# The first context's loads, the last groups' additions and the norm rows of a two-layer cross-attention kernel

## The chip, the core and the metric

The kernel runs on one NeuronCore of a Trainium2 chip, in a single launch. The metric is the device time of one execution in microseconds (us). The profile is one execution taken by the hardware profiler; its span runs from the first to the last instruction.

The engines are named as the profile names them: PE is TensorE (PEld its weight loads), DVE is VectorE, ACT is ScalarE, POOL is GpSimd, SP is the engine whose queue issues every DMA here.

## The reference

There are eight sequences of 512 tokens with 512 features (x), and for each a context of 512 rows with 384 features. Four steps are added to x one after the other, each on a layer-normalised x:

```python
# 1  cosine of projected tokens and projected context rows (H = 256); 512x512 per sequence
v = ln(x) @ Wv.T + bv;  t = ctx @ Wt.T + bt
x = x + (v @ t.T) / max(|v| * |t|, 1e-8)
# 2  ternary feed-forward: quantised activations, ternary weights, 512 -> 2048 -> 512
x = x + bit_linear(silu(depthwise_conv3(bit_linear(ln(x), w1))), w2)
# 3  cross-attention with 16 heads of 32
q = ln(x) @ w_q + b_q;  k = ctx @ w_k + b_k;  u = ctx @ w_v + b_v
x = x + softmax(q @ k.T / sqrt(32)) @ u @ w_o + b_o
# 4  gated channel mixing of each token with the one before it
y = ln(x); xr = mix(y, shifted y, mu_r); xk = mix(y, shifted y, mu_k)
x = x + sigmoid(xr @ W_r) * (relu(xk @ W_k) ** 2 @ W_v)
```

All arrays are float32.

## The kernel before

**Who sets the order.** The kernel is written as small generator tasks (`load`, `split_sb`, `evacuate`, `summed` and so on). While the program is built, an `Agenda` plays them against a plan of the machine: a task yields an engine and a cost ("P" TensorE, "V" VectorE, "A" ScalarE, "G" GpSimd, "S" SP's queue), a kind of buffer, or an event, and the planner takes the waiting task with the lowest rank. The order in which the planner starts the work is the order in which each engine's instructions stand in the program; on the chip each engine runs its list in that order and waits on semaphores. So every number of the plan, such as the delay between an engine's end and the next task (`HOP`), can move many instructions. "W" is VectorE work that shares a memory port with GpSimd in the plan: the two take turns there. Where a task offers a list of ways, as `tensor` does for additions (VectorE or GpSimd), the planner picks the one that is least burdened. Almost every VectorE and GpSimd instruction is issued through one wrapper, so the profile puts them all on line 363; the tiles tell them apart. All ordinary loads and stores go through `load` (line 510).

**Buffers.** SBUF is cut into pages ("main", "small"), PSUM into eight banks ("bank"). A kind of buffer has a limit of how many may be held: `b_mm`, the banks of the projections and cosines of step 1, has five.

**Step 1.** For each sequence `b`, `contexts` loads the context (three chunks of 128 features by 512 rows) and splits each chunk into a rounded high part and a low part (`split_sb`: a cast and a subtraction). For the first sequence the three chunks are loaded one by one, each split before the next is asked for. `fronts` loads x, normalises it and transposes it (line 549). `projections` makes the context side with three products for each pair of parts (lines 456 to 458) and then the x side in float32 (line 448). `evacuate` writes the squares and the values, `norms` sums the squares down the features on TensorE (line 877), and `inverse` raises the sums to the power -1/2 on GpSimd. The norms of the context rows stand down the partitions, one column for each 128 rows; `spread` turns them into a row that stands in all partitions, by four transposes of broadcast columns on TensorE (line 605) and a copy on ScalarE (line 608). `cosines` makes the 512x512 products in four banks (line 448); `finish` on VectorE needs that row, scales each bank, adds x and stores the result as x1. Until `finish` has read it, a bank stays held.

`spread` is also called for the scales of step 2, there without the argument that this change sets, and has a second form, chosen with `through`: store the columns to a DRAM tensor `rd`, then load it as one row broadcast to all partitions.

**Step 3.** Attention runs over 32 groups `n` (eight sequences by four groups of four heads). For each, scores are made with the keys on the partitions (line 1480), exponentials taken on ScalarE (line 1488), and `summed` adds up the exponentials of the four key blocks, in two halves of 128x1024, three additions each. `weigh` multiplies by the values (line 1522). The column sums of the added exponentials (line 1540) of group n - 1 stand ahead of the products of group n; those of the last group stand behind them. `finish3` divides and splits, and the output projection follows.

**Step 4** begins under the end of step 3: `mixed` makes the token mixes (a scaling, a scaled addition on VectorE, a cast, a subtraction), `keys4` multiplies them by W_k (lines 456 to 458 again).

The lines of `contexts` and of `summed` that the change touches, and the callers, are these:

Of the kernel before, what the change touches and what calls it, by code (L numbers as in the profile page):

```python
# [12 lines left out]
ALU = mybir.AluOpType  # L13
# [3 lines left out]
P = 128  # L17
B, S, D = 8, 512, 512
# [3 lines left out]
NCX = DCTX // P  # L22
# [7 lines left out]
NS = B * NG  # L30
# [145 lines left out]
class Agenda:  # L176
# [5 lines left out]

    HOP = {"P": 0.2438, "V": 0.12, "A": 0.17, "G": 0.08, "S": 0.1}

    def __init__(self):
        self.now = self.end = self.lane = self.port = 0.0
# [109 lines left out]
    def dispatch(self, engine):  # L298
        if self.wanted[engine] and self.free[engine] <= self.now:
# [9 lines left out]
            self.busy[engine] += cost  # L309
            self.hop = self.HOP[engine]  # L310
            self.me = task
# [63 lines left out]
def f32(ap):  # L375

    return ap.bitcast(F32)


def tile_kernel(tc, x, ctxT, vecs, bo, wvT, wtT, w1T, w2T, wqkvo, wrT, wkT, wv2T, out):  # L380
    nc = tc.nc
    A, T = nc.scalar, nc.tensor
# [39 lines left out]
    ag = Agenda()  # L422
    V, G = Ported(tc, ag, nc.vector), Ported(tc, ag, nc.gpsimd)
# [49 lines left out]
    def tensor(out, a, b, op):  # L473

        n = a.free_size() / 512
        way = yield [("W", 0.07 + 0.53 * n), ("G", 0.16 + 1.07 * n)]
        (V, G)[way].tensor_tensor(out, a, b, op)

    def copy(out, src):

        n = src.free_size() / 512
        way = yield [("W", 0.07 + 0.27 * n), ("A", 0.10 + 0.42 * n)]
        V.tensor_copy(out, src) if way == 0 else A.copy(out, src)  # L483
# [20 lines left out]
    def split_sb(hi, lo, src):  # L504
        yield from copy(hi, src)
        yield from tensor(lo, src, f32(hi), ALU.subtract)

    def load(dst, src):
        yield "S", 0.5
        nc.sync.dma_start(dst, src)  # L510
        yield ag.transfer(src)
# [78 lines left out]
        for t in range(NT):  # L590
            ag.spawn(part(t), ag.me.rank)

    SPR = 0

    def spread(krow, bank, vals, through=None):

        if through is not None:
            yield from store(rd[through].rearrange("(t p) -> p t", p=P), vals)
            row = yield krow
            yield from load(row, rd[through].unsqueeze(0).to_broadcast([P, S]))  # L600
            return row
        ps = yield bank
        yield "P", 0.44
        for t in range(NT):
            T.transpose(ps[:, t, :], vals[:, t : t + 1].to_broadcast([P, P]), ident)
        row = yield krow
        yield "A", 0.48
        A.copy(row, ps.rearrange("p t q -> p (t q)"))  # L608
        ag.give(ps)
        return row  # L610
# [153 lines left out]
    lns, css, vts = {}, {}, {}  # L764
    ln_done = [Event(NT) for _ in range(B)]
    cd_done = [Event() for _ in range(B)]
    cs_done = [Event() for _ in range(B)]
    vt_done = [Event(2 * NHX) for _ in range(B)]
    ns_done = [Event() for _ in range(B)]
    kv_done = [Event(NG + NT) for _ in range(B)]  # L770
# [24 lines left out]
    def contexts():  # L795
        for b in range(B):
            ag.me.rank = (b - LEAD) * T1
            craw = yield k_ctx
            cs = yield k_cs
            css[b] = cs  # L800
            if b > 0:
                yield from load(craw, ctxT[b])
            for c in range(NCX):
                if b == 0:

                    yield from load(craw[:, c, :], ctxT[b, :, c])
                yield from split_sb(cs[c], cs[NCX + c], craw[:, c, :])
            ag.give(craw)
            ag.set(cs_done[b])
            ag.spawn(parked(b, cs), ag.me.rank)  # L810

    def projections():
        yield w_done["t"]
        for b in range(B):
            ag.me.rank = b * T1
            vv = yield k_vv
            vts[b] = vv
            ns, ns_got, sq_done = [], Event(), Event(2)
            for s in (1, 0):
                if s == 1:  # L820
                    yield cs_done[b]
                    (w,), nk, bias, src = wt, NCX, "bt", css[b]
                else:
                    yield w_done["v"]
                    yield ln_done[b]
                    (w,), nk, bias, src = wv, NC, "bv", lns[b][0]
                sqs, both = [], Event(NHX)
                for m in range(NHX):
                    ps = yield b_mm
                    if s == 1:  # L830
                        yield from mac3(ps, lambda c: parts(w, c, tok(m)), lambda c: part2(src, c, ALL), nk)
                    else:
                        yield from mac4(ps, lambda c: w[:, c, tok(m)], lambda c: src[:, c, :], nk)
                    ag.spawn(evacuate(b, s, m, ps, bias, sqs, both), ag.me.rank)
                ag.spawn(norms(s, sqs, both, ns, ns_got, sq_done), ag.me.rank)
                if s == 0:
                    ag.give(src)
                else:
                    ag.spawn(released_when(cd_done[b], src), ag.me.rank)
            ag.spawn(inverse(b, ns, sq_done), ag.me.rank)  # L840

    def parked(b, cs):

        for i in range(2 * NCX):
            yield from store(cd[b, i // NCX, :, i % NCX], f32(cs[i]))
        ag.set(cd_done[b])
# [34 lines left out]
    def inverse(b, ns, sq_done):  # L881
# [14 lines left out]
        V.tensor_scalar(lim, lim, 1e8, None, ALU.mult)  # L896
        rt = yield from spread(k_row, b_pt, rn[:, NT : 2 * NT], (b, 0) if SPR & 1 else None)
        rns[b] = rn, rt, lim
# [365 lines left out]
    R3 = 620.0  # L1264
    T3 = 19.0
    NSTK = 4
    AVK = 2
    MX = 1.6
    GQ = 5
# [14 lines left out]
    k3_xo = main.kind(2, D)  # L1284
    k3_stk = main.kind(2 * NSTK, HG, S, dtype=F32R)
    k3_nmT = small.kind(2, 2, P, dtype=F32R, rows=HG * NT)
# [7 lines left out]
    b3_av = psum.kind(2, S)  # L1294
    free3 = small.kind(NSTK, 1)
    qk_scale = 1.0 / float(HD) ** 0.5
# [15 lines left out]
    def stacks_made():  # L1312


        for i in range(NSTK):
            qs = yield k3_stk
# [63 lines left out]
    def stacks():  # L1380
        yield stks_done
        for n in range(NS):
# [4 lines left out]
            token = yield free3  # L1387
            qs, ks = stks[n % NSTK]
            tokens[n] = token
# [13 lines left out]
    def maxima():  # L1403

        for n in range(NS):
            ag.me.rank = R3 + (n - MX) * T3
            yield loaded[n]
            qs, ks = stks[n % NSTK]
            nmc = yield s3_nmc
# [16 lines left out]
    def lower_rows(n, nmc, done):  # L1426
        qs, ks = stks[n % NSTK]
        yield done
        pt = yield b3_n
        yield "P", 0.15  # L1430
        T.transpose(pt, nmc.rearrange("p j t -> p (j t)"), ident)
        ag.give(nmc)
        nmT = yield k3_nmT
        yield "A", 0.16
        A.copy(nmT[:, 0, :], pt)
        yield "V", 0.16
        V.tensor_tensor(nmT[:, 1, :], pt, f32(nmT[:, 0, :]), ALU.subtract)
        ag.give(pt)
        for a in range(2):
            yield "S", 0.5  # L1440
            nc.sync.dma_start(f32(qs[96 + a : 97 + a]), f32(nmT[:, a, :]))
            wait = ag.transfer(nmT[:, a, :])
        yield wait
        ag.give(nmT)
        ag.set(max_done[n])
# [46 lines left out]
    def summed(n, h, ps, accs):  # L1492

        for k in range(NT):
            ag.me.rank = R3 + (n + (2 * k + h + 1) / 8) * T3
            yield ps[k, h][1]
            if k == 0:
                acc = yield k3_acc
                accs[h] = acc
            else:  # L1500
                yield from tensor(acc, ps[0, h][0] if k == 1 else acc, ps[k, h][0], ALU.add)
                if k == 1:
                    ag.set(ps[0, h][2])
                ag.set(ps[k, h][2])
        ag.set(accs_done[n])

    def weigh(n, av, ps, av_done):
        for first in range(0, NT, AVK):
            both = [(k, h) for k in range(first, first + AVK) for h in range(2)]
            for k, h in both:  # L1510
                yield ps[k, h][1]
            ag.me.rank = R3 + (n + (2 * (first + AVK) - 1) / 8) * T3
            before = n > 0 and first == 0
            if before:
                yield accs_done[n - 1]
                sm = yield b3_w
            yield "P", 0.31 + 0.863 * (AVK + before)
            if before:
                sums(n - 1, sm)
            for k in range(first, first + AVK):  # L1520
                for j in range(HG):
                    T.matmul(  # L1522
                        av[j * HD : (j + 1) * HD, :], vs[n][:, k, j * HD : (j + 1) * HD],
                        ps[k, j // 2][0][:, j % 2, :], start=(k == 0), stop=(k == NT - 1),
                    )
            for k, h in both:
                ag.set(ps[k, h][2])
                ag.spawn(released(*ps[k, h]), ag.me.rank)
        ag.set(av_done)
        ag.give(vs.pop(n))  # L1530
        if n == NS - 1:
            yield accs_done[n]
            sm = yield b3_w
            yield "P", 1.17
            sums(n, sm)
# [307 lines left out]
```

## Time and profile before

| | us |
|---|---|
| three runs | 1606.19, 1607.86, 1610.59 |
| their median | 1607.86 |
| the profiled execution, its time | 1610.36 |
| its span, first to last instruction | 1608.4 |
| PE busy | 1542.0 (96% of the span) |
| DVE busy | 1241.1 (77%) |
| ACT busy | 1090.9 (68%) |
| POOL busy | 671.8 (42%) |
| mean granted TensorE clock | 0.988 |

Busy time is the time in which the engine had an instruction running; register and DMA-issuing instructions do not count. An engine's idle time is put down to what released the instruction after it. The steps overlap: step 1 fills about 0 to 225 us (beside the keys and values of step 3 and the start of step 2), step 2 runs to about 710, attention from about 720 to 1300, step 4 from there to the end.

### The profile page before, as it was taken

How to read it: one execution, taken by the hardware profiler on the slowest of the kernel's cores; microseconds unless marked ns; L12 is line 12 of the kernel's file. 1: busy time of each engine (PE TensorE's matmuls, PEld its weight loads, DVE VectorE, ACT ScalarE, POOL GpSimd, SP SyncE). 2: the span in 40 equal slices, each digit the busy share in tenths (PEclk: the TensorE clock that was granted, in tenths of full speed). 3: DMA queues.
4: the chain of work that ended last, by engine and by line, in shares of the span. 5: the costliest groups of instructions: out<-in, count | busy, mean ns of one | idle time of the engine just before them, and what ended most of it. 6: DMA issues, size and time to landing. Idle time of an engine off the chain costs nothing.

```text
span 1608.4 us, 22301 instructions
## 1 busy us (share of the span) xinstructions
PE 1542.0 (96%) x7552; PEld 987.3 (61%) x7552; DVE 1241.1 (77%) x2044; ACT 1090.9 (68%) x1794; POOL 671.8 (42%) x385
## 2 busy tenths in 40 slices
PE   6999999998999998989999999999999979999998
PEld 4555566655566665656666556555555547878886
DVE  5678899999789989869885887788987555655642
ACT  6686889868778887645766666666676665656551
POOL 1111000000000000133867889988878994544540
PEclk9999999999999999999999999999999989999999
DMA  8898524443444444577666666565765232112101
GB/s 301 309 360 279 180 86 130 151 145 123 159 132 144 148 136 149 191 258 219 183 181 191 177 151 179 144 180 157 197 170 147 74 90 101 52 60 69 69 27 53
DMA packets 133395, 251.48 MB, mean 156 GB/s; under 512 B 22689, under 2 KB 40481, under 8 KB 127138
## 3 DMA queue, kind: packets, MB, share of 16 engines
q1 hardware_dynamic: 133282, 250.06, 49.6%
q8 instruction: 60, 0.98, 0.3%
q14 instruction: 53, 0.43, 0.1%
HBM read 160.88 MB, written 88.34 MB: 155 GB/s over the span
## 4 chain that ended last, share of the span: by engine, by line
PE 68%; DVE 19%; DMA 4%; ACT 4%; issue 3%; POOL 1%; SPq 0%; POOLq 0%; ACTq 0%; DVEq 0%
DVE main L363 15%; PE bank L456 10%; PE bank L457 9%; PE bank L458 9%; PE bank L1480 7%; PE bank L1416 7%; PE bank L1522 6%; PE bank L1218 5%; PE bank L448 4%; DVE small L363 4%; PE bank L442 3%; PE bank L549 2%; PE bank L1540 2%; PE bank L1142 2%; ACT main L1488 1%
## 5 line engine op out<-in xcount | busy, mean ns | idle before, releaser
L363 POOL TENSOR_TENSOR main<-main,main 128x1024 f32<-128x1024 f32 (+3 forms) x316 | 588.5, 1886 | 255.5 <-DVE main L363 96.9
L456 PE MATMUL bank<-main,main 128*128 128x512 f32 x874 | 390.7, 447 | 13.5 <-ACT main L608 3.6
L363 DVE TENSOR_REDUCE small<-bank 128x1 f32<-128x512 f32 (+2 forms) x522 | 330.3, 675 | 89.1 <-PE bank L1416 86.1
L1488 ACT ACTIVATE main<-bank 128x512 f32<-128x512 f32 x512 | 279.4, 604 | 103.2 <-PE bank L1480 99.1
L458 PE MATMUL bank<-main,main 128*128 128x512 f32 x874 | 345.6, 395 | 0.0
L457 PE MATMUL bank<-main,main 128*128 128x512 f32 x824 | 326.3, 396 | 3.5 <-POOL main L363 2.9
L363 POOL TENSOR_TENSOR small<-small,mhalf 128x4 f32<-128x4 f32 (+2 forms) x43 | 51.2, 1191 | 644.8 <-DVE small L363 627.8
L363 DVE TENSOR_TENSOR main<-main,main 128x1024 f32<-128x1024 f32 (+3 forms) x205 | 245.8, 1209 | 16.5 <-ACT main L483 8.0
L456 PEld LDWEIGHTS bank<-main,main 128*128 128x128 f32 x874 | 166.8, 191 | 87.5 <-issue 22.3
L1480 PE MATMUL bank<-main,main 98*128 98x512 f32 x512 | 212.8, 418 | 2.8 <-ACT main L1488 1.2
L1416 PE MATMUL bank<-main,main 96*128 96x512 f32 x512 | 211.2, 414 | 1.5 <-DVE small L363 0.4
L458 PEld LDWEIGHTS bank<-main,main 128*128 128x128 f32 x874 | 165.9, 190 | 37.2
L363 DVE SCALAR_TENSOR_TENSOR main<-bank,vec,main 128x511 f32<-128x511 f32 x254 | 181.5, 740 | 7.8 <-ACT main L1148 7.4
L457 PEld LDWEIGHTS bank<-main,main 128*128 128x128 f32 x824 | 157.7, 191 | 34.1 <-issue 3.9
L442 PE MATMUL bank<-main,main 128*128 128x512 fp8e4 x512 | 134.2, 388 | 3.4 <-ACT main L1124 3.4
L483 ACT CAST main<-main 128x512 fp32r<-128x512 f32 x168 | 102.4, 633 | 50.3 <-POOL main L363 17.5
L1480 PEld LDWEIGHTS bank<-main,main 98*128 98x128 f32 x512 | 96.4, 188 | 60.9 <-ACT main L1488 16.3
L1416 PEld LDWEIGHTS bank<-main,main 96*128 96x128 f32 x512 | 96.5, 189 | 42.3 <-DVE small L363 11.1
L1522 PE MATMUL bank<-main,main 128*32 128x512 f32 x968 | 122.5, 595 | 0.0
L1218 PE MATMUL bank<-main,main 128*128 128x512 fp8e4 x456 | 120.7, 384 | 0.0
L1148 ACT ACTIVATE main<-bank,vec 128x512 f32<-128x512 f32 x128 | 100.0, 788 | 16.0 <-PE bank L1142 15.0
L1124 ACT ACTIVATE main<-bank,small 128x512 f32<-128x512 f32 x128 | 87.2, 700 | 17.3 <-PE bank L442 16.9
(110 smaller groups left out, 1996.4 us busy)
## 6 DMA issues: line engine op xcount, KB each, us to landing
x<-main SPq DMA_DIRECT2D x96, 256.0 KB
main<-x SPq DMA_DIRECT2D x24, 1024.0 KB
kd<-main SPq DMA_DIRECT2D x32, 512.0 KB
main<-x SPq DMA_DIRECT2D x64, 256.0 KB
qd<-main SPq DMA_DIRECT2D x32, 512.0 KB
main<-kd SPq DMA_DIRECT2D x32, 512.0 KB
main<-qd SPq DMA_DIRECT2D x32, 512.0 KB
cd<-main SPq DMA_DIRECT2D x48, 256.0 KB
```

Source lines behind the costliest of these rows:

```text
L363: ins = call(*args, **kwargs)
L442: T.matmul(ps, lhs(c), rhs(c), start=(c == 0), stop=(c == n - 1))
L456: T.matmul(ps, lh, rh, start=(c == 0), stop=False)
L457: T.matmul(ps, lh, rl, start=False, stop=False)
L458: T.matmul(ps, ll, rh, start=False, stop=(stop and c == n - 1))
L483: V.tensor_copy(out, src) if way == 0 else A.copy(out, src)
L1148: A.activation(g, ps, AF.Identity, bias=col("cb", f), scale=col("cw", 3 * f + 1))
L1218: T.matmul(po, qs[f // 2][:, f % 2, tok(t)], w2q[f // 8][:, f % 8, :], start=(f == 0), stop=(f == NF - 1))
L1416: T.matmul(ps, qs[0:96, j, tok(t)], ks[0:96, j, :], start=True, stop=True)
L1480: T.matmul(ps, ks[0:98, 2 * h + i, tok(k)], qs[0:98, 2 * h + i, :], start=True, stop=True)
L1488: A.activation(p, ps, AF.Exp, scale=qk_scale)
L1522: T.matmul(av[j * HD : (j + 1) * HD, :], vs[n][:, k, j * HD : (j + 1) * HD], ps[k, j // 2][0][:, j % 2, :], start=(k == 0), stop=(k == NT ...
```

## The change

There are three edits and one constant of the plan.

- The loads and splits of the first context's three chunks become three tasks of their own (`context0`), all started at once. `contexts` then waits for an event that counts the chunks. In the program that results, SP issues the weights first, then the three chunks one behind the other, then x; before, it issued chunk 0, the weights, x, chunk 1, the second sequence's x, chunk 2.
- `SPR = 1` makes `inverse` call `spread` with `through`: for each of the eight sequences the norm row goes by a store of 128x4 single elements to `rd` and a broadcast load of 256 KB. The scales of step 2 keep the transposes. TensorE's 32 transposes and ScalarE's 8 copies for these rows are gone, and SP has 16 more issues.
- With `LASTS = 2`, the additions of the last two of the 32 groups are made on VectorE alone; the planner may no longer give them to GpSimd. Twelve additions of 128x1024 are concerned.
- The plan's delay behind TensorE work is 0.2487 instead of 0.2438. With the edits this makes the planner order the whole program anew, with small differences throughout.

```diff
-    HOP = {"P": 0.2438, "V": 0.12, "A": 0.17, "G": 0.08, "S": 0.1}
+    HOP = {"P": 0.2487, "V": 0.12, "A": 0.17, "G": 0.08, "S": 0.1}
...
-    SPR = 0
+    SPR = 1
...
-    cs_done = [Event() for _ in range(B)]
+    cs_done = [Event(NCX) for _ in range(B)]
...
             for c in range(NCX):
                 if b == 0:
-                    yield from load(craw[:, c, :], ctxT[b, :, c])
-                yield from split_sb(cs[c], cs[NCX + c], craw[:, c, :])
+                    ag.spawn(context0(c, craw, cs), ag.me.rank)
+                else:
+                    yield from split_sb(cs[c], cs[NCX + c], craw[:, c, :])
+                    ag.set(cs_done[b])
+            yield cs_done[b]
             ag.give(craw)
-            ag.set(cs_done[b])
             ag.spawn(parked(b, cs), ag.me.rank)
+
+    def context0(c, craw, cs):
+        yield from load(craw[:, c, :], ctxT[0, :, c])
+        yield from split_sb(cs[c], cs[NCX + c], craw[:, c, :])
+        ag.set(cs_done[0])
...
+    LASTS = 2
...
             else:
-                yield from tensor(acc, ps[0, h][0] if k == 1 else acc, ps[k, h][0], ALU.add)
+                one = ps[0, h][0] if k == 1 else acc
+                if n < NS - LASTS:
+                    yield from tensor(acc, one, ps[k, h][0], ALU.add)
+                else:
+                    yield "W", 1.13
+                    V.tensor_tensor(acc, one, ps[k, h][0], ALU.add)
```

## The prediction, made before the changed kernel ran

> **What bounds the kernel now.** First the page's busy line and the windows (columns of a window: its length, then busy time and instructions of PE, PE's weight loads, DVE, ACT and POOL, then the granted clock, the DMA engines' busy share and GB/s).
>
> ```profile
> PE 1542.0 (96%) x7552; PEld 987.3 (61%) x7552; DVE 1241.1 (77%) x2044; ACT 1090.9 (68%) x1794; POOL 671.8 (42%) x385
> ```
> ```profile
> 0.00:30.00 30.00, 14.83 (x64) 11.13 (x65) 18.20 (x54) 16.53 (x27) 5.66 (x14) 1.00 0.82 278
> 30.00:50.00 20.00, 20.00 (x83) 12.34 (x82) 11.78 (x27) 17.73 (x33) 2.65 (x2) 1.00 0.98 349
> 90.00:130.00 40.00, 40.00 (x167) 23.75 (x166) 28.59 (x66) 30.07 (x53) 5.27 (x4) 0.99 0.89 335
> ...
> 300.00:500.00 200.00, 187.70 (x974) 114.74 (x972) 180.79 (x295) 159.59 (x229) 3.02 (x3) 0.98 0.45 145
> ...
> 1290.00:1325.00 35.00, 26.89 (x107) 16.94 (x105) 22.47 (x26) 22.91 (x41) 32.59 (x20) 0.80 0.31 92
> ```
>
> TensorE is the bound nearly everywhere: 1542 of 1608.4 us busy. What can be had is its 66 us of gaps, or work taken off it. The change touches two of the larger gaps: 15.2 us in the first 30, and 8.1 us in 1290 to 1325, where the clock also fell to 0.80. A third, 12.3 us in 300 to 500 (VectorE 90% busy there), it does not touch by design. From 30 to 170 the DMA engines are almost as full as TensorE, and that matters for the added transfers.
>
> Second, the timeline of the start (start, duration, engine, line).
>
> ```profile
> 8.59 0.38 SPq L510 DMA_DIRECT2D main<-in_x  x1
> 9.26 0.69 DVE L363 BATCH_NORM_STATS2 small<-main 128x6 f32<-128x512 f32 x1 [2.73 <-DMA main<-in_x]
> 9.32 0.33 SPq L510 DMA_DIRECT2D cd<-main  x1
> ...
> 13.68 1.12 PE L549 MATMUL bank<-ident,main 128*128 128x128 f32 x4 [13.68 <-ACT main L498]
> ...
> 18.95 0.34 PEld L456 LDWEIGHTS bank<-main 128*128 128x128 f32 x1
> ...
> 19.44 0.33 SPq L510 DMA_DIRECT2D main<-in_ctxT  x1
> ```
>
> TensorE starts with x's transposes at 13.68. The first projection (line 456) waits until 18.95 for the third context chunk, and the SP queue issues nothing from 9.65 to 19.44, because its next load waits for the buffer that this chunk occupies.
>
> Third, who waited for whom on TensorE from 1250 to 1335, and GpSimd's timeline there.
>
> ```profile
> PE bank L1540 <- POOL main L363: 4.4, 2, 3.0
> PE bank L457 <- POOL main L363: 2.9, 1, 2.9
> ```
> ```profile
> 1287.92 7.08 POOL L363 TENSOR_TENSOR main<-main,main 128x1024 f32<-128x1024 f32 x3
> 1295.46 10.03 POOL L363 TENSOR_TENSOR main<-main,main 128x1024 f32<-128x1024 f32 x5 [0.46 <-ACT main L496]
> ```
>
> The last exponential ends at 1294.10, but GpSimd, at about 2.4 us an addition, is still adding until 1300.9. The sums (line 1540) wait 4.4 us for it, and the next stage's first products (line 457) 2.9 us more, for a subtraction queued behind the additions.
>
> **The first context.** SP's new order is weights, three chunks, x. Before, 1.5 MB were issued up to the end of x's first tile, which landed at 9.26, and the trace then moves about 0.3 MB per us. Now 0.96 MB of weights and vectors lie ahead of the chunks; by that rate they land at about 8.5, 9.4 and 10.4, and x's first tile, which ends at 2.0 MB, at 11.2. The third chunk's cast and subtraction (0.62 and 0.69) end at 11.8; eighteen products at the cold pace of 0.43 us take 7.7 us, fifteen of them ahead of the first transpose in the new order. x's own chain then begins after 11.8 and is some 2.5 us late: its transposes start at 16 to 17 instead of 13.68. ScalarE now has in one row four normalisations (0.8), four copies of transposes (0.59), four evacuations (0.7) and a cast (0.64): about 9 us from 15.9, so the value projection of the first batch starts at 24 to 24.7 instead of 26.5. By the instruction order it is followed by eight halves of 0.86 and four transposes of 0.43, 8.6 us, until the second batch's context projection at 32.9 instead of 33.97. That is 1.1 us gained. Ends: 5.4 us gained (the whole context projection out of the way), or 2 lost (all that x comes later). I take 1.1, the end of the followed chain. The 9.8 us hole of SP's queue goes too, but TensorE is what is full next.
>
> **The norm rows by DRAM.** Eight groups of four transposes on line 605 go from TensorE: 41.18 to 41.54, 0.36 us each, 2.9 us in all (ends 0, if a DMA is what is late, and 4, with the 1.1 us that a product waited for a row's copy). Eight ScalarE copies of 0.59 go, 4.7 us, off the path. Added are sixteen issues of 0.45 on SP, 7 us of a queue that mostly waits, and 2.1 MB for the broadcast rows, 6 us at 335 GB/s, in a stage with over 10% of DMA free, about 15 us from 30 to 170: taken at nothing; 6 if that cover is gone. The store has 512 four-byte pieces, and the trace has no such. The nearest row, the reciprocals' store of 128 pieces of 64 B, lands in 1.41 us; four times that, 5.6, is its upper end, nothing the lower, in which other stores hide it.
>
> What counts is how late the row comes: the copy through TensorE took 2 us, and four banks of cosines wait for it. Before the first bank is needed again (the second batch's value projection), the new order puts twelve halves of 0.86, twelve products of 0.23, three transposes of 0.43 and 0.85 of norm products: 15.2 us; for the next batch it is 17.8. The chain is 2.2 (maximum, power), store, load, 0.75 (finish). With the quiet landings of 1.41 and 2.06 it is 6.4; with the 6.45 that a 256 KB store took at 69.77 for each, 15.9; with the 8.21 of 133.67, 19.4. A tiny store behind some pending ones lies nearer the first two: 9 to 13, covered. I take 0; ends 0 and 8 × 4.2 = 34. In SP's order up to four issues lie between store and load, in the last two batches one and none. The load waits there for the store's landing, and behind it queue context stores, weight loads and x1 stores; with up to seven earlier transfers in flight, the engines have work meanwhile.
>
> The Trainium skill's page "DMA: Bandwidth & Descriptors", section "Rules for kernel authors", speaks against this part: a strided last dimension becomes one descriptor per element. Its section on the anatomy of one DMA puts about 2.0 us fixed on each transfer; by that, as an estimate, the quiet pair would take 4.0 where the two rows give 3.47, and the sum would not move. No row here shows one descriptor per element.
>
> **The last two groups.** The new order does have all twelve additions on VectorE, so the edit does what it says. GpSimd loses eleven of 2.4 (one was VectorE's already), 26 us, in a stretch where it was 36.8 of 40 busy. VectorE gets twelve of 1.3 to 2.3, the slow ones beside a running GpSimd: 16 to 27 us, where it idled 20 of 40 us. After the last exponential at 1294.1 come one scaling (0.55 to 1.9) and one addition (1.1 to 2.1), so the sums end at 1297.2 to 1299.4 instead of 1302.9. The mixes that feed the next stage stand behind them on VectorE: four of 0.73 to 1.5, then a cast of 0.62 and a subtraction of 1.28 on a GpSimd that is now free. TensorE is dense from about 1304 instead of 1309. I take 5 us; ends 1 (only the sums move, the mixes do not) and 10 (all of the 8.1 us gap and the 2 us of cold pace).
>
> **The planner's new hop** (0.2487) only reorders. VectorE loses nine casts (0.416) to ScalarE and five scalings, and gains seven casts and some additions: about nothing. Unknown to me: some gaps of 300 to 755 open or close; 6 us either way.
>
> **Sum**, against the profiled execution's own 1610.36 us (span 1608.4): 1.1 + 2.9 + 0 + 5.0 = 9.0, giving 1601.4. That execution lies 2.5 above the median of 1607.86, so the forecast is 1599.
>
> **The rivals.** Slower, the row comes late: it decides when store and load together take over 15.2 − 2.95 = 12.2 us. At 7.3 each (between the two landings seen) each batch loses 2.4 us while the banks are held, 19 for eight; against 9 gained that is 1618. For it: transfers of 6.45 and 8.21 us in just this stage. Against: SP's queue spends 64 of 170 us waiting for VectorE, so the queue in front is often short.
>
> No change: the additions move the wait instead of ending it, since VectorE's mixes at 1.5 to 2 us beside GpSimd come as late as before. Then the tail gives 1, line 605 2.9 and the start nothing: 1604.
>
> Much faster: the tail gives 8, the start 4, line 605 3, and reordering 3: 1590.
>
> **How the numbers follow.** Forecast 0.45, much faster 0.15, no change 0.15, late row 0.25. About 0.3%, 4.8 us, is what a measurement of this kernel can tell from none. The first two lie beyond it on the fast side: faster 0.60; same 0.15; slower 0.25. The range takes the forecast's 9 with its 6 either way, then reaches into both rivals: 1586 to 1618.
>
> **What would show it.** Right: the first product of line 456 at about 12 and the second batch's near 33; no instruction of line 605 before 170 us, and no new TensorE wait for VectorE there; the wait of the sums for GpSimd gone and the 1290 to 1325 gap below 4 us. Wrong: TensorE waiting in the first 230 us for line 363's finishes or the loads from rd, or the gap before the last stage as long as before, now ended by VectorE.

## The result, and the profile after

The changed kernel takes 1653.64 us (median of five runs, 1651.9 to 1655.92) against 1608.17 for the kernel before in the same comparison (1606.19 to 1611.16): a ratio of 1.028, 95% interval 1.0262 to 1.0298. It is 45 us slower, where 9 us of gain were forecast, and it lies outside the stated 1586 to 1618.

First the changed kernel's busy line, then its windows (columns as before: length, busy time and instructions of PE, weight loads, DVE, ACT, POOL; granted clock, DMA share, GB/s).

```profile
PE 1558.1 (94%) x7520; PEld 988.8 (60%) x7520; DVE 1247.3 (75%) x2050; ACT 1094.6 (66%) x1793; POOL 643.5 (39%) x370
```
```profile
0.00:30.00 30.00, 19.24 (x64) 11.93 (x65) 17.49 (x50) 16.61 (x28) 4.72 (x14) 0.89 0.88 312
30.00:50.00 20.00, 20.00 (x84) 12.46 (x83) 8.71 (x22) 15.76 (x30) 3.77 (x3) 1.00 0.92 193
50.00:90.00 40.00, 28.56 (x95) 15.15 (x93) 21.44 (x48) 18.77 (x29) 4.92 (x3) 0.94 1.00 294
90.00:130.00 40.00, 37.34 (x140) 22.45 (x141) 27.09 (x60) 32.97 (x53) 4.50 (x3) 0.89 0.99 316
```

The start is better filled, as planned: 19.24 busy us in the first 30 instead of 14.83. From 30 to 50 comes the first sign of trouble, and it isn't on TensorE, which is still full: the DMA engines stand at 92% and move 193 GB/s, where they moved 349 before at 98%. From 50 to 90 TensorE has work for 28.56 of 40 us (36.73 before), with the DMA engines at 100%.

The timeline around the first norm row shows the place: SP's queue, then one ten-microsecond window before and after the change, then who waited on VectorE, on SP and on TensorE up to 240 us (a waits line gives the total, how often, and the longest).

```profile
38.42 0.38 SPq L510 DMA_DIRECT2D rd<-small  x1
...
39.89 0.92 SPq L510 DMA_DIRECT2D cd<-main  x2
47.78 0.32 SPq L510 DMA_DIRECT2D main<-rd  x1
```
```profile
40.00:50.00 10.00, 10.00 (x43) 6.04 (x42) 6.66 (x15) 8.49 (x16) 1.01 (x1) 1.00 0.94 328
```
```profile
40.00:50.00 10.00, 10.00 (x36) 5.60 (x35) 2.42 (x4) 6.37 (x13) 0.00 (x0) 1.00 1.00 62
```
```profile
DVE main L363 <- DMA main<-rd: 15.1, 2, 8.8
```
```profile
SPq L510 <- DMA rd<-small: 46.6, 6, 10.6
```
```profile
PE bank L448 <- DVE main L363: 10.0, 3, 4.1
```

The store of 2 KB is issued at 38.42, and the load of the row can follow only at 47.78, 9.4 us later. In the ten microseconds from 40 the DMA column reads 100% and the rate 62 GB/s. At the 328 GB/s of the kernel before in the same window that traffic takes 1.9 us; about 8 us are gone. Over all eight batches it is 8.4 to 16.8 us from the store's issue to that of its load. SP waits 46.6 us for such stores in six places, and every load and store of the stage stands behind it. TensorE's cosine and value products wait 10.0 us for VectorE, a wait that the kernel before does not have there.

The start and the tail, in TensorE's timeline (bracketed: the idle time before, and what ended it):

```profile
8.10 0.80 PE L456 MATMUL bank<-main 128*128 128x512 f32 x1 [8.10 <-ACT main L483]
...
14.78 0.66 PE L549 MATMUL bank<-ident,main 128*128 128x128 f32 x4 [0.24 <-ACT main L498]
...
32.62 0.80 PE L456 MATMUL bank<-main,main 128*128 128x512 f32 x1
...
1339.71 2.05 PE L1554 MATMUL bank<-main,ones 128*32 128x512 f32 x8
...
1344.49 0.50 PE L457 MATMUL bank<-main,main 128*128 128x512 f32 x1 [1.96 <-POOL main L363]
...
1364.21 0.66 PE L549 MATMUL bank<-ident,main 128*128 128x128 f32 x4 [3.26 <-ACT main L498]
```

TensorE begins 5.6 us earlier, and with the context. The last sums (now line 1554, at 1339.71) wait for nobody, and follow the last exponential, which ended at 1338.69, by 1 us; before, the first of them came 4 us and the rest nearly 7 us behind it. But step 4's first products and transposes wait again (1.96 and 3.26).

The loss is made in step 1 and carried to the end: the last cosine products start 43 us later than before (279.24 instead of 236.10), the span ends 46 later. The stretch up to these products, before and after the change:

```profile
0.00:236.00 236.00, 215.41 (x892) 129.22 (x893) 179.78 (x380) 177.19 (x277) 29.04 (x30) 0.99 0.72 254
```
```profile
0.00:279.00 279.00, 229.70 (x872) 132.57 (x873) 181.56 (x381) 176.15 (x272) 29.87 (x30) 0.92 0.78 222
```

Of the 43 us, 28.7 are more idle time of TensorE (49.3 instead of 20.6). The other 14.3 are busy time: it has 20 matmuls fewer and takes longer for them, with a mean granted clock of 0.92 instead of 0.99.

### The profile page after: what moved, and what is told of

Same layout as the page of the kernel before. It is cut to its first block, busy times and chain, and to the rows that moved or that the text cites. A ratio compares the mean times of both kernels' runs of the same rounds, so it can differ in the third digit from the quotient of the medians.

```text
span 1654.1 us, 22277 instructions
## 1 busy us (share of the span) xinstructions
PE 1558.1 (94%) x7520; PEld 988.8 (60%) x7520; DVE 1247.3 (75%) x2050; ACT 1094.6 (66%) x1793; POOL 643.5 (39%) x370
## 5 line engine op out<-in xcount | busy, mean ns | idle before, releaser
L363 POOL TENSOR_TENSOR main<-main,main 128x1024 f32<-128x1024 f32 (+3 forms) x290 | 538.1, 1880 | 237.9 <-DVE main L363 106.3
L363 DVE TENSOR_TENSOR main<-main,main 128x1024 f32<-128x1024 f32 (+4 forms) x217 | 255.9, 1187 | 41.7 <-ACT main L1183 10.9
L442 PE MATMUL bank<-main,main 128*128 128x512 fp8e4 x512 | 136.7, 392 | 4.9 <-ACT main L1131 4.5
L483 ACT CAST main<-main 128x512 fp32r<-128x512 f32 (+1 forms) x163 | 98.7, 623 | 53.8 <-POOL main L363 22.3
L1225 PE MATMUL bank<-main,main 128*128 128x512 fp8e4 x512 | 132.0, 381 | 1.3 <-DVE main L363 1.3
```

Of the source, the lines that this page charges most:

```text
L363: ins = call(*args, **kwargs)
L442: T.matmul(ps, lhs(c), rhs(c), start=(c == 0), stop=(c == n - 1))
L1225: T.matmul(po, qs[f // 2][:, f % 2, tok(t)], w2q[f // 8][:, f % 8, :], start=(f == 0), stop=(f == NF - 1))
```

## The experiments

All ratios are to the kernel before, run beside each kernel (medians 1607.4 to 1608.4), with a 95% interval.

### Which edit loses the time

**e1_spr0**: the changed kernel with transposed norm rows.

```diff
-    SPR = 1
+    SPR = 0
```

> The changed kernel with the norm rows spread by TensorE's transposes again (SPR = 0), all else as changed; the planner orders it anew. Theory S (the store of 512 four-byte pieces keeps the DMA engines busy for about 9 us each time, and everything behind it waits): the loss goes, 1600 to 1612 us. Rival O (the new order of the whole program, by the hop and the other edits, costs much of it): stays above 1625.

Measured: 1606.74 us, 0.9997 [0.9987, 1.0007]. **e2_only_spr** is the reverse, the kernel before with `SPR = 1` alone:

> The kernel before with SPR = 1 alone. Theory S: 1645 to 1665 us, as slow as the changed kernel. Rival O: below 1625.

Measured: 1668.7, 1.0387 [1.036, 1.0414], a little above its range. The DRAM rows lose 46.9 us with the other edits (1653.64 − 1606.74) and 61 without them. All the rest of the change comes to nothing; why, is taken up below.

### A late row, or engines that are held?

**e4_store_alone** is the kernel before, rows through TensorE as ever, with eight stores added that nobody reads:

```diff
+        yield from store(rd[b, 0].rearrange("(t p) -> p t", p=P), rn[:, NT : 2 * NT])
         rt = yield from spread(k_row, b_pt, rn[:, NT : 2 * NT], None)
```

> The kernel before with eight stores of 512 four-byte pieces added ahead of the transposes that still spread the rows; nothing loads what they write, but the row's transposes stand behind the planned landing of the store. Theory S in its pure form (the engines are held, whoever waits for the row): 1635 to 1655 us. Rival R (the row's lateness alone): under 1620.

Measured: 1654.96, 1.03 [1.0272, 1.0327]. No product, no load and no `finish` uses what these stores write, and still 47.5 us are lost (1654.96 − 1607.43). SP's queue waits only 8.3 us for them up to 240 us. So the loss does not need a late row. One thing this run does not keep apart: the planner sets the row's transposes behind the store, and the program's order differs from that of before from its 111th matmul on. That the stores hold up the other transfers does not rest on this run alone: e3_16byte, without a change of order, and the packets further down show it too. Two windows of this kernel soon after the first store, which is issued at 38.65:

```profile
44.00:46.00 2.00, 2.00 (x9) 1.13 (x8) 0.69 (x1) 0.65 (x2) 0.00 (x0) 1.00 0.58 49
46.00:48.00 2.00, 2.00 (x10) 1.14 (x9) 0.00 (x0) 0.00 (x0) 0.00 (x0) 1.00 0.66 63
```

49 and 63 GB/s, although loads and context stores were issued up to 44.5 and wait to be moved.

**e3_16byte** keeps the whole change and the order of its instructions, and lays the row out in DRAM so that each partition's four values stand side by side: 128 pieces of 16 bytes. `finish` reads the row with a stride instead.

```diff
-            yield from store(rd[through].rearrange("(t p) -> p t", p=P), vals)
+            yield from store(rd[through].rearrange("(p t) -> p t", p=P), vals)
...
```

> The changed kernel, instruction for instruction in the same order, but the store of the norms writes four neighbouring elements for each partition (128 pieces of 16 bytes instead of 512 of 4), and the finish on VectorE reads the row through a strided view. Theory S: a store takes a quarter or less, so SP's waits for it fall from 46.6 to under 15 us, and the time falls by 25 to 45 us, to 1609 to 1629. Rival R (the round trip store, wait, load in SP's queue is what costs, whatever the pieces): over 1640.

Measured: 1616.06, 1.006 [1.004, 1.0079]. The same bytes, the same order on every engine, a quarter of the pieces: 37.6 us of the changed kernel's time go, of the 46.9 that the DRAM rows cost it. The row comes sooner too, so this run by itself does not part a late row from held engines. SP's wait for the row's store up to 240 us falls from 46.6 to

```profile
SPq L510 <- DMA rd<-small: 13.0, 6, 5.4
```

**g2_rows** goes to four pieces of 512 bytes, by one TensorE transpose to 4x128 and a small ScalarE copy:

```diff
-            yield from store(rd[through].rearrange("(t p) -> p t", p=P), vals)
...
+            T.transpose(ps[:NT, 0, :], vals, ident)
...
+            A.copy(row[:NT, :P], ps[:NT, 0, :])
...
+            yield from store(rd[through].rearrange("(t p) -> t p", p=P), row[:NT, :P])
```

> The changed kernel with the norm row put through DRAM in four pieces of 512 bytes: the 128x4 norms are transposed to 4x128 by one TensorE instruction, copied by ScalarE, stored, and loaded as before. If it is the small pieces that hold the DMA engines: 1605 to 1609, at the kernel without the DRAM rows (1606.7) or below it, since 24 transposes of 0.09 us are gone. If the broadcast loads and the queue's wait between store and load cost by themselves (the 16-byte form was still 9 us above that kernel): 1612 to 1618.

Measured: 1612.6, 1.0028 [1.0015, 1.0041], in the second range. The small pieces were the bulk of the loss, but the DRAM way did not pay here even without them: 5.9 us above e1_spr0.

The page's row for the one queue that carries nearly all transfers (packets, MB, and the time that all packets took, as a share of sixteen engines' span) shows the stores a second time. In order: before, changed, e4_store_alone, e3_16byte, g2_rows.

```profile
q1 hardware_dynamic: 133282, 250.06, 49.6%
```
```profile
q1 hardware_dynamic: 138658, 252.18, 51.6%
```
```profile
q1 hardware_dynamic: 137506, 250.08, 51.0%
```
```profile
q1 hardware_dynamic: 135586, 252.18, 50.9%
```
```profile
q1 hardware_dynamic: 134498, 252.18, 50.6%
```

Share times span is the packets' time added up and divided by sixteen: 49.6% of 1608.4 is 797.8 us before, 51.0% of 1651.5 is 842.3 in e4_store_alone. The eight stores came with 44.5 us more, 5.6 each, and the packets rose by 4224, or 528 a store: the 512 elements and sixteen more. The sum is sure to some 6 us, or more with the broadcast loads: e1_spr0 and f1_context, with no such transfer added, lie 4 and 6 above before, and e2_only_spr and h2_after_old_hop, with the same transfers, at 851 and 865. So the 24 of e3_16byte and the 16 of g2_rows, which hold the eight broadcast loads too, give no price for a store of larger pieces.

Whose time the 44.5 us are, the single packets of the trace tell. The pieces have hardly any of it: all four-byte packets of e4_store_alone together took 12.1 us of sixteen engines, those of before 9.4, and one takes 0.009 us (median). It is the packets of the other transfers that last longer. Those of this queue over 2 us, in the first 300 us:

| kernel | packets over 2 us | their time / 16 | longest packet |
|---|---|---|---|
| before | 0 | 0 | 1.68 us |
| changed | 111 | 22.8 us | 8.30 us |
| e4_store_alone | 100 | 19.6 us | 5.94 us |
| e3_16byte | 0 | 0 | 1.96 us |
| g2_rows | 0 | 0 | 1.94 us |

None of them is of four bytes. All five kernels with the four-byte stores have such packets (65 to 148), and none of the nine other kernels. In the changed kernel the 528 packets of the first store begin between 39.0 and 40.0 us; from 40 to 50 there are 15.8 packets in flight on average, one for each engine, and packets of 4 KB, whose median is 0.16 us, last up to 8.30. So the engines are held, but by other transfers that do not get on while the store has yet to land. Why they do not, no run here shows.

**h4_plan_knows** tells the planner the price, so that it can order around it:

```diff
...
+            ag.lane = max(ag.lane, ag.end + 0.6) + 8.0
...
```

> The changed kernel, where the plan is told that each of the eight four-byte stores holds the transfers for 8 us (instead of next to nothing), so that it can order loads ahead and products around them. If the loss came of the plan's ignorance: 1615 to 1630. If it is lack of DMA time (8 x 8 = 64 us asked of a stage that has about 15 free): 1645 to 1660.

Measured: 1654.48, 1.0286 [1.0268, 1.0303]. The last cosine products start 12 us sooner than in the changed kernel, and by the end nothing is left of it. That fits a stage that is short of DMA time, but does not show it.

### Where the expected gain went

Now the other edits by themselves. **f1_context** is the kernel before with the first context's three tasks, **f2_lasts** the kernel before with `LASTS = 2`, **h1_hop_only** the kernel before with the constant 0.2487, **g1_hop** the changed kernel with `SPR = 0` and the old constant, that is, the two edits together:

```diff
-    HOP = {"P": 0.2487, "V": 0.12, "A": 0.17, "G": 0.08, "S": 0.1}
+    HOP = {"P": 0.2438, "V": 0.12, "A": 0.17, "G": 0.08, "S": 0.1}
...
-    SPR = 1
+    SPR = 0
```

> The kernel before with the first context's three tasks as its only edit (old plan constant, transposed norm rows, additions as before). My sum gave this edit 1.1 us of gain. If leads made early in the kernel are kept to the end: 1606 to 1607 against 1607.4. If they are eaten in the planner's gaps between 300 and 1000 us, as the kernel without the DRAM rows suggests (its cosines ended 8 us earlier and its attention 2 us earlier): between 1605 and 1610, that is no difference.

> The kernel before with only the last two groups' additions on VectorE. My sum gave it 5 us. If that holds: about 1602. If the wait only changes its place, as my rival of no change had it (in the full change the sums came 5.4 us earlier relative to the last exponential, and the first 31 us of step 4 then idled 5.9 us instead of 0.6): 1606 to 1608, the sums' wait for GpSimd gone and a new TensorE wait on line 549 or 457 of 4 to 5 us in the first 40 us after the sums.

> The kernel before with the plan's constant 0.2487 as its only change. With the two useful edits the old constant was 9 us faster than the new one (1597.7 against 1606.7). If the constant by itself makes a worse order: about 1617. If it only met these edits badly: 1605 to 1611, as before (1608.4).

> The changed kernel with transposed norm rows and the old plan constant 0.2438: the two useful edits alone. If the edits are worth what my sum says (6.1 us): about 1601. If they are worth nothing and the constant changed nothing either: 1605 to 1609, like the kernel with the new constant (1606.7). A difference from that kernel is what the reordering by the constant is worth; I gave it 6 us either way.

| kernel | time | ratio, 95% interval |
|---|---|---|
| f1_context | 1601.05 | 0.9952 [0.9935, 0.997] |
| f2_lasts | 1609.38 | 1.0004 [0.999, 1.0018] |
| h1_hop_only | 1615.52 | 1.0052 [1.0035, 1.007] |
| g1_hop | 1597.7 | 0.9935 [0.9919, 0.9952] |

The context edit is worth 7.4 us, not 1.1; its time lies below both ranges. The tail edit alone is worth nothing that can be measured; on top of the context edit 3.4 us (1601.05 − 1597.7, within the spread of both). The constant costs 7.8 us alone and 9.0 with the two edits (1606.74 − 1597.7): nearly the 10.7 that they gain together, which is how e1_spr0 came out at nothing. **g1_hop, faster than either of its ranges, beats both the kernel before and the changed one.**

Landmarks, in us (start of the last rows of cosine products; load of the table for the first exponential; start of the very last column sum; end of the span):

| kernel | cosines | exponentials | last sums | end |
|---|---|---|---|---|
| before | 236.1 | 748.3 | 1301.8 | 1608.4 |
| changed | 279.2 | 792.8 | 1341.2 | 1654.1 |
| e1_spr0 | 227.7 | 743.8 | 1294.6 | 1607.7 |
| f1_context | 224.4 | 732.8 | 1291.2 | 1601.8 |
| f2_lasts | 234.0 | 744.6 | 1292.0 | 1606.2 |
| g1_hop | 224.8 | 731.8 | 1287.4 | 1597.8 |
| h1_hop_only | 231.4 | 751.8 | 1303.3 | 1614.1 |

f2_lasts has the order of before up to the end of step 2, so its 2 and 4 us in the first two columns show how far two executions differ. Its last column is the reading that matters: from the sums to the end takes 314.2 us, and before 306.6. Of 9.8 us by which the sums came sooner, 2.2 are left at the end of this execution, and none in the medians. In its own profile the sums no longer wait for GpSimd; TensorE waits instead, from 1280 to 1360, for the normalised x of step 4:

```profile
PE bank L549 <- ACT main L498: 4.7, 1, 4.7
...
PE bank L457 <- POOL main L363: 1.5, 1, 1.5
```

In e1_spr0 the constant's loss arises in step 2 (from the cosines to the exponentials 516 us in e1_spr0, 507 in g1_hop), in part where line 1149 waits for VectorE. First e1_spr0, then g1_hop, both from 227 to 745 us:

```profile
PE bank L1149 <- DVE main L363: 12.7, 11, 3.5
```
```profile
PE bank L1149 <- DVE main L363: 8.0, 10, 2.0
```

### Do the parts add up?

**h2_after_old_hop** is the changed kernel, four-byte stores and all, with the old constant; **h3_rows_old_hop** is g2_rows with the old constant.

> The changed kernel with the old constant 0.2438, all three edits kept. If the parts add up: 1653.6 minus the 9 us that the constant cost without the DRAM rows, 1644.6. If the DRAM rows override what the order gains early, because the stage up to 240 us is then set by the held DMA engines: 1651 to 1658, as with the new constant.

> The norm row by DRAM in four pieces of 512 bytes, with the old constant: the DRAM way at its cheapest, beside 1597.7 for the transposed rows. If the DRAM way can pay once its pieces are large (24 short transposes less): 1595 to 1597. If broadcast loads, queue waits and a later row cost more than the 2 us of TensorE that they free: 1600 to 1606.

Measured: 1680.78, 1.0451 [1.0436, 1.0467], and 1624.54, 1.0092 [1.0073, 1.0111]. Both theories of both runs are missed, and on the same side. With the DRAM rows the constant that costs 9 us elsewhere saves 27 (1680.78 − 1653.64) or 12 (1624.54 − 1612.6). So parts do not add up over reorderings, and a difference of some 10 us between two of these kernels is not yet the price of an edit. That is also the limit on e3_16byte and g2_rows: with g2_rows the order changed along with the size of the pieces, with e3_16byte it did not. Why the old order meets the DRAM rows so badly (from the cosines to the exponentials 529 us in h2_after_old_hop, 514 in the changed kernel) stays open.

## Why the prediction was wrong, point by point

**The step that failed is the store's term.** "The store has 512 four-byte pieces, and the trace has no such"; its landing was bounded by 0 and 5.6 us, as a delay of the row, and its effect on the other transfers was never put into the sum: "taken at nothing" covered the issues and the broadcast loads, and for the wait behind the store the text said "the engines have work meanwhile". Measured, the engines were held and moved 62 GB/s instead of 328. Eight such stores by themselves (e4_store_alone) cost 47.5 us and lengthened the packets' time by 44.5 us of all sixteen engines, in a stage for which the text itself counted about 15 us of free DMA time. The bound on the landing was too low as well: the load behind the store was issued 8.4 to 16.8 us after it.

Would a row of before have given it? 49.6% of 1608.4 us on sixteen engines for 133282 packets is 0.096 us of one engine per packet, of 1.9 KB on average. At that price, 512 pieces cost 3.1 us of all sixteen engines and eight stores 25 us, over the cover of 15: a warning, but not by the right quantity, since the trace of before has 14225 four-byte packets at 0.009 us each, by which a store costs 0.3 us. What such a store does to the transfers beside it stood in no row. The row of 128 pieces of 64 B, taken four times, said how long the requester might wait, and nothing on this.

The Trainium skill's page "DMA: Bandwidth & Descriptors", section "Rules for kernel authors", had the rule that bears on this: a strided last dimension becomes one descriptor per element. The packet count agrees, with 528 a store. The prediction weighed that rule by the 2.0 us fixed per transfer of the page's section on the anatomy of one DMA, which is written for transfers issued by GpSimd, where here SP issues them. The measurement, 9.4 us from the first store's issue to that of the load behind it, shows that this was the wrong way to weigh it.

**The rival of the late row** had the right place and part of the mechanism. Its condition came true: the pair of store and load was to take over 12.2 us, and in four of the eight batches the store alone held its load back for longer. `finish` waits 15.1 us for the row up to 240 us, TensorE 10.0 us for VectorE, one of the named signs of being wrong, and e2_only_spr, where the row is needed, is 14 us above e4_store_alone, where it is not (in another order). But 47.5 us are lost where nothing needs the row from DRAM, and its price was 19. The evidence against it, that SP's queue in front is often short, missed the point: a short queue of SP does not show how full the engines are. One of its readings was off: the store at 69.77 had landed by its sixteenth semaphore update after 7.60 us, not 6.45; neither bound rests on it.

**The row's cover** of 15.2 us is the sum of its terms, but products cannot cover a wait when the transfers that feed them are late too.

**The first context**: direction right, size wrong. The first product of line 456 started at 8.10 (forecast about 12), the first batch's value projection at 21.35 (forecast 24 to 24.7), and the second batch's context projection at 32.62 (forecast 32.9). But that one product was no measure of the edit. TensorE's gaps in the first 30 us fell by 4.4 (19.24 busy us instead of 14.83, some of them at a lower clock), other work had moved ahead of that product, and f1_context, where it starts at 31.33, has the cosines 11.7 us earlier and the end 7.4. The upper end of 5.4 lies just inside the interval of that gain (4.8 to 10.5), the 1.1 far outside.

**Line 605**: right; its first instruction in the changed kernel is at 282.1. The 2.9 us are too small to be seen beside the rest.

**The tail**: the mechanism was right up to the sums, and they no longer wait for GpSimd. What came next was not the mixes, as the rival of no change had it, but step 4's fill. In the changed kernel's first 31 us of dense products (the second line is the gap that was to be under 4 us, moved by the 44 us of delay):

```profile
1348.70:1379.70 31.00, 25.14 (x105) 19.16 (x106) 20.32 (x22) 21.99 (x38) 27.15 (x19) 0.94 0.31 100
...
1334.00:1369.00 35.00, 27.83 (x115) 18.33 (x113) 25.85 (x34) 27.72 (x48) 25.62 (x17) 0.90 0.40 126
```

5.9 us idle, where the same stretch before (1309 to 1340) had 0.6, and 7.2 in the 35 us around the sums instead of 8.1. In f2_lasts the 5.0 of the sum measured nothing. That rival's end, a wait that only moves, was right for this edit.

**The constant**: "about nothing, 6 either way" was 7.8 to 9.0 slower without the DRAM rows, and 12 to 27 faster with them.

In steps from kernel to kernel the loss is −10.7 us for the two edits (1597.7 against 1608.4), +9.0 for the constant and +46.9 for the rows, +45.2 in all. That it adds up is no proof, since each step starts where the last one ended; by another path the single numbers would differ, as the runs with the old constant show.

## What to carry to other kernels

A store in short pieces is priced neither by its bytes, nor by its landing, nor by the time of its own packets: what counts is what it does to the transfers beside it. To see that, put such a store by itself into the kernel before, and read the rate in its window and how long the other packets last. It cost this much in a stage whose DMA engines were 76 to 98% busy before. An edit that shortens a wait is worth what is left at the end: name the next wait in line before counting the gain. And where a planner orders the program, try an edit with and without the constants that came with it, since here one constant undid nearly all that the edits gained.

## What the runs showed of the hardware

- Eight stores of 512 four-byte pieces each from SBUF to DRAM, 2 KB in all a store, raised the packet count by 528 a store and the time of all packets by 44.5 us of sixteen engines. The four-byte packets themselves took 0.009 us each (2.7 of the 44.5 us); while such a store was under way, packets of 2 and 4 KB of other transfers lasted up to 8.30 us. With 128 pieces of 16 bytes or four of 512 bytes no packet of the same queue lasted 2 us in the first 300.
- In the window of such a store the DMA column read 100% at 62 GB/s, against 94% at 328 GB/s in the same window before. A high DMA share is not a high rate: the two columns have to be read together. The column counts a packet's whole time where the packet begins; from 40 to 42 us it reads 2.69.
